# Two fused transformer blocks on one core: layer 0's down product of batches 1 to 3 split into exact fp32r passes, gate weights asked for by ScalarE, next norm moved

## The chip, the cores and the metric

One core of a Trainium2 chip runs the whole program. The metric is the device time of one execution in microseconds (us). Three runs of the kernel before took 1489.95, 1476.10 and 1484.36 us, median 1484.36.

## The reference, cut to what matters

Four batches of 512 tokens with 512 features go through two layers. In each, `x = x + attention(norm(x)) * silu(ffn(norm(x)))`. Layer 0 is what changes:

```python
xn = layernorm(x)
s = softmax_attention(xn) @ Wo                 # 32 query heads, 8 key heads, head size 16
h = silu(xh @ W_gate.T * sg) * (xh @ W_up.T * su)   # xh = Hadamard(xn * SU_ug), 2048 wide
y = Hadamard(h * SU_dp) @ W_down.T * sd        # 2048 -> 512: the "down product"
x = x + s * silu(y)
```

Layer 1 has a gated delta-rule recurrence with six heads of 64 as its attention, and an FFN whose weights are signs. It is not changed. The Hadamard transforms are folded into the weights on the chip, so that the down product of one batch is a 2048 by 512 matrix `wdn` times the hidden `hT` (features by tokens, 16 tiles of 128x512).

## The kernel before

**Units.** Layer 0 is a loop over units u = 0 to 267 (`for u in range(NU + LAG + 1)`, NU = 256, LAG = 11, LATE = 16). A unit takes one step of every stage:

- `maxima(u)` (L461, L462): two score matmuls into the one PSUM buffer "sc", and a DVE reduction of them to row maxima.
- `exps(u - 11)` (L486, L488): two transposed score matmuls into the one PSUM buffer "st", and one ACT exponential of 128x1024.
- work that earlier units postponed with `later(n, f)`, n units on.
- at u % 8 = 3, `values` (L496, L502 to L521): sixteen matmuls of probabilities by values into "y". The row sums go through DRAM (L503, L505), DVE inverts them (L509), they come back spread out (L510, L512), POOL multiplies (L516), and four copies place the result (L521).
- two halves of an FFN unit v = u - 16.
- at set units: query rows (L475, L477), queries (L423, L427, copied by L448), the layer sum of the batch before (`layer_sum`, L534 to L539), its second norm (stats1, `norm1_turn` L568 to L571), and for the next batch `load_x`, norm0 (stats0 L137, root L146 to L154, scale L73, turn L166, copy L167), `keys` (L319, L322, L328) and `values_of` (L341, L346).

**FFN units.** A batch b has 64 of them. In the first 32 (`gate_up`) each unit makes one half of a 128x512 tile of gate or up: eight fp32r matmuls (L363), four 128-row parts of the features by a high and a low half of the weights. ACT takes the tanh of the gate (L370), DVE makes the silu (L371, one unit later), ACT copies the up product into `hT` (L374) and POOL multiplies the two (L375). In the other 32 (`down`) each unit makes two fp32 matmuls (L382) of a 128-token slice of `hT` by `wdn[:, c]`. After sixteen of them ACT takes a tanh (L386) and DVE writes the gate `g0` (L387), tokens by features. FFN units run 16 behind u, so in the loop's own count r = u % 64 the down units stand at r = 48 to 63 and 0 to 15, and the gate units at r = 16 to 47. The text calls them the down stretch and the gate stretch. After u = 255 one half goes to each unit, and what remains of batch 3 (`rest`) is mixed with the first projections of layer 1.

**Weights.** Batch 0 folds the weights as it goes (`fos`) and stores the gate and up weights, split in two, in DRAM (`wS`). For batches 1 to 3 `gate_weights` (L579) loads one 512 KB tile "wc" for each gate unit, three units ahead, through SP's queue; four buffers. `wdn` stays in SBUF and is folded by `fold_down` (L301, L302).

**Order.** From u = 48 `keep_order()` ties every instruction of PE, DVE, ACT and POOL to the one before it on its engine, in the order in which the Python code issues them. SP, which issues nearly all DMAs, is not tied by it; its queue is in order, and an issue waits for its data there.

**PSUM.** "mm" has three buffers, "sc", "st" and "y" one each. `misc()` gives "y" to values, query rows, queries, keys, values_of, the norms' transposes and layer_sum.

Of the kernel before, what the change touches and what calls it, by code (L numbers as in the profile page):

```python
# [10 lines left out]
F32 = mybir.dt.float32  # L11
# [19 lines left out]
EPS = 1e-5  # L31
GUESS = 1597463007.0
# [3 lines left out]
def kernel(ctx: ExitStack, tc: tile.TileContext, i: dict, out: bass.AP):  # L36
# [53 lines left out]

    identf = new(cst, [P, P], F32, "identf")
# [9 lines left out]
    if True:  # L101
# [10 lines left out]
        wdn = new(awp, [P, NI, DM], F32, "wdn")  # L112
# [81 lines left out]
        stage = [new(hp, [P, DM], F32, "hT", bufs=16) for _ in range(NI)]  # L194
# [93 lines left out]
        def mix_down(q):  # L288
# [4 lines left out]
            if q == NI - 1:  # L293
                for o in range(4):
                    nc.sync.dma_start(
                        wdn[:, ts(o, 4), :], wdt[ts(o, DM), :].rearrange("(a p) n -> p a n", p=P)
                    )

        def fold_down(a):
            ph = misc()  # L300
            nc.tensor.matmul(ph, hmat, wdn[:, a, :], start=True, stop=True)  # L301
            nc.vector.scalar_tensor_tensor(wdn[:, a, :], ph, cdn[:, a : a + 1], drow, ALU.mult, ALU.mult)  # L302
# [53 lines left out]
        def gate_up(b, c, m, part):  # L356
# [15 lines left out]
            else:  # L372
                hT = hTs[b, c] = new(hp, [P, SEQ], F32, "hT", bufs=16)
                nc.scalar.copy(hT, pgs[1])  # L374
                nc.gpsimd.tensor_tensor(hT, hT, ths[b, c], ALU.mult)  # L375

        def down(b, t, c):
# [4 lines left out]
            nc.tensor.matmul(ys[t], hTs[b, c][:, ts(t, P)], wdn[:, c, :], start=(c == 0), stop=(c == NI - 1))  # L382
# [5 lines left out]

        def ffn(u, part):
            b, r = u // 64, u % 64  # L390
            if r < 32:
                gate_up(b, r // 2, r % 2, part)
            else:
                down(b, (r - 32) // 8, 2 * (r % 8) + part)
# [135 lines left out]
        def layer_sum(b, t):  # L530
            tok = ds((b * TB + t) * P, P)
            ps = misc()
            for k in range(KC):
                nc.tensor.matmul(ps, oTs[b, k][:, ts(t, P)], wo[:, k, :], start=(k == 0), stop=(k == KC - 1))  # L534
            def place():
                sg = new(zp[0], [P, DM], F32, "sg")
                nc.vector.scalar_tensor_tensor(sg, ps, 0.5, g0s[b][:, t, :], ALU.mult, ALU.mult)
                x1 = x1s[t] = new(zp[0], [P, DM], F32, "x1", bufs=4)
                nc.gpsimd.tensor_tensor(x1, sg, xins[b][:, t, :], ALU.add)  # L539
                nc.sync.dma_start(x1_d[tok, :], x1)  # L540
# [34 lines left out]
        def gate_weights(p):  # L575
            b, r = p // 64, p % 64
            if 0 < b < NB and r < 32:
                w = wcs[b, r // 2, r % 2] = new(zp[0], [P, 2, KC, P], F32R, "wc", bufs=4)
# [1004 lines left out]
```

## Time and profile before

| | |
|---|---|
| runs | 1489.95, 1476.10, 1484.36 us; median 1484.36 |
| profiled execution | 1483.26 us, of which the span on the core is 1481.5 |
| mean granted TensorE clock | 0.990 |
| PE busy | 1413.0 us (95%) |
| DVE, ACT, POOL busy | 1039.4, 691.0, 313.9 us |
| batch 1: gate stretch, down stretch | 265.91 to 361.96, 361.96 to 441.96 us |
| batch 2 | 441.96 to 534.32, 534.32 to 615.78 us |
| batch 3 | 615.78 to 706.14; layer 1's first matmul at 778.02 us |
| DMA | 199.10 MB, mean 134 GB/s |

How lines of the profile are read. A group has the line, the engine, the operation, output<-inputs by the program's names, shapes and a count; then the busy time and the mean ns of one; then the idle time of the engine just before them and what ended it. A timeline line has the start, the length, the engine, the line and the count of instructions drawn together, and in brackets the idle time before it with what ended it. PE is TensorE's matmuls, PEld its weight loads; SPq is SP's sequencer, which issues DMAs. "DMA share" is the mean busy share of the core's 16 DMA engines.

### The profile page before, as it was taken

To read this page: it belongs to the slowest core of one execution; us is meant where nothing else is said; L and a number is where in the kernel's file an instruction comes from. 1 tells how busy PE (TensorE), PEld (TensorE's weight loads), DVE (VectorE), ACT (ScalarE), POOL (GpSimd) and SP (SyncE) were. 2 spreads that over 40 slices of the span, in tenths; PEclk is the share of its full clock that TensorE was granted. 3 is DMA by queue.
4 is the path that set the end of the run, shared out by engine and by line. 5 is a ranking of instruction groups with operands and counts; after the bars stand their busy time and mean duration, and the time that the engine had idled before them with its cause. 6 is when DMAs were issued, how large, how long until landed. Compare 5 with 4: busy or idle time off the path is not lost.

```text
span 1481.5 us, 22721 instructions
## 1 busy us (share of the span) xinstructions
PE 1413.0 (95%) x8144; PEld 856.0 (58%) x8144; DVE 1039.4 (70%) x1926; ACT 691.0 (47%) x1027; POOL 313.9 (21%) x304
## 2 busy tenths in 40 slices
PE   7989999989999999999999799999999999999898
PEld 3555533555335643466334566777568766776675
DVE  7999755767557755676517769677965799477646
ACT  4654454556445664566443424423442345323433
POOL 1122200323004210133111220054112531152001
PEclk9999999999999999999999999999999999999989
DMA  8865220465006730266024443434462354425532
GB/s 304 329 224 191 101 73 23 160 228 193 25 23 210 236 132 25 74 226 212 20 61 124 149 114 100 131 77 149 126 177 83 97 155 134 128 72 153 157 82 96
DMA packets 201792, 199.10 MB, mean 134 GB/s; under 512 B 65520, under 2 KB 153040, under 8 KB 200784
## 3 DMA queue, kind: packets, MB, share of 16 engines
q1 hardware_dynamic: 198624, 196.29, 42.0%
q10 hardware_dynamic: 3056, 1.37, 0.4%
q8 instruction: 64, 1.05, 0.3%
q14 instruction: 48, 0.39, 0.1%
HBM read 146.80 MB, written 46.19 MB: 130 GB/s over the span
## 4 chain that ended last, share of the span: by engine, by line
PE 64%; DVE 22%; DMA 5%; issue 4%; ACT 3%; SPq 1%; POOL 1%; POOLq 0%; ACTq 0%; DVEq 0%
PE mm L382 15%; PE mm L363 12%; PE ph L1066 5%; PE sc L461 4%; PE y L1097 4%; DVE yc L844 2%; DVE UT L1200 2%; PE pu L885 2%; DVE sx L1196 2%; DVE nmx L462 2%; PE pu L836 1%; PE pu L1157 1%; PE pu L1333 1%; PE pu L1306 1%; PE pu L1394 1%
## 5 line engine op out<-in xcount | busy, mean ns | idle before, releaser
L462 DVE TENSOR_REDUCE nmx<-sc 128x2 f32<-128x1024 f32 x256 | 312.7, 1222 | 194.4 <-PE st L486 192.4
L488 ACT ACTIVATE pe<-st 128x1024 f16<-128x1024 f32 x256 | 262.3, 1024 | 158.9 <-PE st L486 157.9
L382 PE MATMUL mm<-wdn,hT 128*128 128x512 f32 x512 | 253.5, 618 | 0.0
L363 PE MATMUL mm<-xr,wc 128*128 128x512 f32 x768 | 205.6, 410 | 7.5 <-DMA wc<-wS 7.2
L363 PEld LDWEIGHTS mm<-xr,wc 128*128 128x128 f32 x768 | 138.5, 190 | 57.8 <-issue 27.4
L375 POOL TENSOR_TENSOR hT<-hT,th 128x512 f32<-128x512 f32 x64 | 84.9, 1326 | 291.2 <-ACT hT L374 285.2
L382 PEld LDWEIGHTS mm<-wdn,hT 128*128 128x128 f32 x512 | 87.0, 189 | 93.4 <-issue 93.1
L836 PE MATMUL pu<-xn1T,wp 128*128 128x512 f32 x288 | 131.2, 599 | 0.0
L1066 PE MATMUL ph<-xsh,sg 128*128 128x512 f32 x256 | 113.7, 444 | 6.0 <-ACT sg L1051 5.7
L516 POOL TENSOR_TENSOR oT<-os,sm 128x512 f16<-128x512 f32 x32 | 41.3, 1292 | 313.8 <-DMA sm<-rec_d 222.9
L1051 ACT ACTIVATE sg<-sw 128x512 fp32r<-128x512 f32 x128 | 79.5, 625 | 56.3 <-PE y L1097 29.0
L1066 PE MATMUL ph<-xsl,sg 128*128 128x512 f32 x256 | 104.9, 410 | 0.7 <-DVE xsl L1026 0.7
L461 PE MATMUL sc<-kT,qT 32*128 32x512 f16 x512 | 99.6, 385 | 5.9 <-DVE nmx L462 5.6
L486 PE MATMUL st<-qm,kT 32*128 32x512 f16 x512 | 100.3, 386 | 0.2 <-ACT pe L488 0.2
L461 PEld LDWEIGHTS <-qT 32*128 32x128 f16 x512 | 25.4, 91 | 120.7 <-issue 115.1
L1071 ACT ACTIVATE hT<-ph,upsc 128x512 f32<-128x512 f32 x64 | 43.8, 684 | 94.2 <-PE ph L1066 94.0
L836 PEld LDWEIGHTS pu<-xn1T,wp 128*128 128x128 f32 x288 | 54.0, 192 | 56.3 <-issue 54.7
L1097 PE MATMUL y<-sg,hsh 128*128 128x512 f32 x256 | 83.3, 434 | 0.6 <-ACT sg L1051 0.6
L1144 POOL TENSOR_TENSOR gm<-g,le 128x384 fp32r<-128x384 f32 x64 | 56.8, 905 | 87.1 <-PE pu L1145 54.7
L363 PE MATMUL mm<-xr,fo 128*128 128x512 f32 x256 | 73.8, 421 | 1.1 <-DVE fo L277 1.1
L1097 PE MATMUL y<-sg,hsl 128*128 128x512 f32 x256 | 73.5, 400 | 0.0
L370 ACT ACTIVATE th<-mm,hwg 128x512 f32<-128x512 f32 x64 | 44.0, 688 | 63.1 <-PE mm L363 63.1
(311 smaller groups left out, 2355.6 us busy)
## 6 DMA issues: line engine op xcount, KB each, us to landing
wc<-wS SPq DMA_DIRECT2D x96, 512.0 KB
wS<-fo SPq DMA_DIRECT2D x16, 1024.0 KB
sw<-in_upT SPq DMA_DIRECT2D x64, 256.0 KB
sw<-in_downT SPq DMA_DIRECT2D x64, 256.0 KB
sm<-rec_d SPq DMA_DIRECT2D x128, 64.0 KB
raw<-in_w_gateT SPq DMA_DIRECT2D x8, 512.0 KB
hT<-in_w_downT SPq DMA_DIRECT2D x16, 256.0 KB
raw<-in_w_upT SPq DMA_DIRECT2D x8, 512.0 KB
```

Of the source, the lines that this page charges most:

```text
L363: nc.tensor.matmul(pgs[m], wcs[b, c, m][:, h, k, :], xrs[b][:, k, :], start=(k + h == 0), stop=(k == KC - 1 and h == 1))
L375: nc.gpsimd.tensor_tensor(hT, hT, ths[b, c], ALU.mult)
L382: nc.tensor.matmul(ys[t], hTs[b, c][:, ts(t, P)], wdn[:, c, :], start=(c == 0), stop=(c == NI - 1))
L461: nc.tensor.matmul(sc[:, j, :], qTs[n][rows, ts(t, P)], kTs[b, g // 4][rows, :], start=True, stop=True)
L462: nc.vector.tensor_reduce(nmxs[n][:, t, 2 * pr : 2 * pr + 2], sc, AX.X, ALU.max, negate=True)
L486: nc.tensor.matmul(st[:, j, :], kTs[b, g // 4][rows, ts(k, P)], qms[n][rows, :], start=True, stop=True)
L488: nc.scalar.activation(pes[u], st, AF.Exp)
L836: nc.tensor.matmul(pp, wps[b, n][:, k, 0:P], xn1Ts[b][:, k, :], start=(k == 0), stop=(k == KC - 1))
L1051: tc.keep_in_program_order(nc.scalar.activation(sgs[b, c, m], raws[b, c, m], AF.Sign))
L1066: ins = nc.tensor.matmul(ph, sgs[b, c, 0][:, ts(k, P)], xss[b][n][:, k, :], start=(k + n == 0), stop=(k == KC - 1 and n == 1))
L1097: ins = nc.tensor.matmul(yss[b][t], hss[b, c][n][:, ts(t, P)], sgs[b, c, 1], start=(c + n == 0), stop=(c == NI - 1 and n == 1))
L1144: nc.gpsimd.tensor_tensor(gm, bc_in(s["g2"][:, t, u, x], P), bc_mid(le, 3), ALU.mult)
```

## The change

It touches layer 0 only.

1. *Down product of batches 1 to 3.* Each 128x128 by 128x512 product in fp32 becomes three passes in fp32r: two in "A" (Wh by Hh, and Wl by Hl, where Wh and Wl are the high and low parts of the weights, Hh that of `hT`, and Hl its low part times 4096), one in "B" (Wl - Wh/4096 by Hh - Hl). A times 1 + 1/4096, plus B, is the whole product. The result has features by tokens. The weights come from two new DRAM arrays, `wA` and `wB`, in 24 tiles of 512 KB a batch, through the "wc" buffers. `down_product` asks for the tile it begins and for the next two, on ACT's queue; the first request of a batch stands directly ahead of its first product. The order of the 192 passes is a fixed list `products`: A for o = 0 and 1; A for o = 2 and 3 together, with B for o = 0 six steps behind (the "joint part"); then the rest of B. While A of o = 3 goes on, DVE subtracts low from high in each of the sixteen `hT` pairs.
2. *Split of `hT`* in the gate stretches of batches 1 to 3. ACT copies the up product, scaled, into "cut"; POOL multiplies (one unit later); DVE masks off low bits in `truncate` (two later); ACT writes the high part and POOL the low part (three later). "hT" gets 32 buffers, and `wdn` becomes sixteen of them.
3. *Batch 0's down stretch* stays in fp32 and makes the parts of the weights: `down_parts`, sixteen times.
4. *layer_sum* of batches 1 to 3 is transposed as well, and the new `token_sum` turns its result with four fp32 transposes and adds x on DVE (POOL for batch 0).
5. *Moved steps.* norm0 of the next batch from r = 36 to 52 to r = 48 to 59, its four stats in two units; `keys` from r = 49 to 60; `values_of` from r = 52, 53, 57, 60 to r = 1, 2, 5, 6 of its own batch; `load_x` from r = 26 to 32; queries seven units ahead instead of ten, their copies four instead of eight; second norm of the batch before by three to six units.
6. *Gate weights* are asked for by ACT instead of SP, with five buffers instead of four.

The diff, cut:

```diff
@@ -88 +89 @@
 
     wdt = new(dram, [FF, DM], F32, "wdt")
 
+    wA = new(dram, [KC, NI // 4, P, 4, 2, P], F32, "wA")
+    wB = new(dram, [KC, NI // 8, P, 8, P], F32, "wB")
+
@@ -191 +194 @@
-        stage = [new(hp, [P, DM], F32, "hT", bufs=16) for _ in range(NI)]
+        stage = [new(hp, [P, DM], F32, "hT", bufs=2 * NI) for _ in range(NI)]
+        wdn = [new(hp, [P, DM], F32, "hT", bufs=2 * NI) for _ in range(NI)]
@@ -291 +295 @@
             if q == NI - 1:
-                for o in range(4):
-                    nc.sync.dma_start(
-                        wdn[:, ts(o, 4), :], wdt[ts(o, DM), :].rearrange("(a p) n -> p a n", p=P)
-                    )
+                for a in range(NI):
+                    nc.sync.dma_start(wdn[a], wdt[ts(a, P), :])
 
         def fold_down(a):
             ph = misc()
-            nc.tensor.matmul(ph, hmat, wdn[:, a, :], start=True, stop=True)
-            nc.vector.scalar_tensor_tensor(wdn[:, a, :], ph, cdn[:, a : a + 1], drow, ALU.mult, ALU.mult)
+            nc.tensor.matmul(ph, hmat, wdn[a], start=True, stop=True)
+            nc.vector.scalar_tensor_tensor(wdn[a], ph, cdn[:, a : a + 1], drow, ALU.mult, ALU.mult)
+
+        def down_parts(a):
+            cut = new(zp[0], [P, DM], I32, "xn1")
+            nc.vector.tensor_scalar(cut, wdn[a].bitcast(I32), -4096, None, ALU.bitwise_and)
+            cut = cut.bitcast(F32).rearrange("p (o n) -> p o n", o=KC)
+            hl = new(zp[0], [P, KC, 2, P], F32R, "wc", bufs=5)
+            low = new(zp[0], [P, KC, P], F32R, "xo")
+
+            def halves_of():
+                nc.scalar.copy(hl[:, :, 0, :], cut)
+                nc.gpsimd.tensor_tensor(
+                    hl[:, :, 1, :], wdn[a].rearrange("p (o n) -> p o n", o=KC), cut, ALU.subtract
+                )
+
+            def difference():
+                nc.vector.scalar_tensor_tensor(low, cut, -CUT, hl[:, :, 1, :], ALU.mult, ALU.add)
+                nc.sync.dma_start(
+                    wA[:, a // 4, :, a % 4].rearrange("o p f n -> p o (f n)"),
+                    hl.bitcast(F32).rearrange("p o f n -> p o (f n)"),
+                )
+                nc.sync.dma_start(wB[:, a // 8, :, a % 8].rearrange("o p n -> p o n"), low.bitcast(F32))
+
+            later(1, halves_of)
+            later(3, difference)
 
@@ -369 +395 @@
                 pg = pgs[0]
                 nc.scalar.activation(th, pg, AF.Tanh, scale=hwg[:, c : c + 1])
                 later(1, lambda: nc.vector.scalar_tensor_tensor(th, th, 1.0, pg, ALU.add, ALU.mult))
-            else:
-                hT = hTs[b, c] = new(hp, [P, SEQ], F32, "hT", bufs=16)
+            elif b == 0:
+                hT = hTs[b, c] = new(hp, [P, SEQ], F32, "hT", bufs=2 * NI)
                 nc.scalar.copy(hT, pgs[1])
                 nc.gpsimd.tensor_tensor(hT, hT, ths[b, c], ALU.mult)
+            else:
+                cut, t = new(hp, [P, SEQ], F32, "cut"), ths[b, c]
+                nc.scalar.activation(cut, pgs[1], AF.Copy, scale=1.0 / CUT)
+
+                def truncate():
+                    nc.vector.tensor_scalar(cut.bitcast(I32), t.bitcast(I32), -4096, None, ALU.bitwise_and)
+
+                def halves_of():
+                    hi, lo = hTs[b, c] = [new(hp, [P, SEQ], F32R, "hT", bufs=2 * NI) for _ in range(2)]
+                    nc.scalar.activation(hi, cut, AF.Copy, scale=CUT)
+                    nc.gpsimd.tensor_tensor(lo, t, cut, ALU.subtract)
+
+                later(1, lambda: nc.gpsimd.tensor_tensor(t, cut, t, ALU.mult))
+                later(2, truncate)
+                later(3, halves_of)
 
         def down(b, t, c):
...
-            nc.tensor.matmul(ys[t], hTs[b, c][:, ts(t, P)], wdn[:, c, :], start=(c == 0), stop=(c == NI - 1))
+            nc.tensor.matmul(ys[t], hTs[b, c][:, ts(t, P)], wdn[c], start=(c == 0), stop=(c == NI - 1))
...
+        dws = {}
+
+        def down_weights(b, n):
+            if n < 16:
+                w = new(zp[0], [P, 4, 2, P], F32R, "wc", bufs=5)
+                nc.scalar.dma_start(w.bitcast(F32), wA[n // 4, n % 4])
+            else:
+                w = new(zp[0], [P, 8, P], F32R, "wc", bufs=5)
+                nc.scalar.dma_start(w.bitcast(F32), wB[(n - 16) // 2, n % 2])
+            dws[b, n] = w
+
+        def tile_of(kind, o, c, f):
+            return 4 * o + c // 4 if kind == "A" else 16 + 2 * o + c // 8
+
+        AHEAD = 6
+        products = [("A", o, c, f) for o in range(KC - 2) for c in range(NI) for f in range(2)]
+        for c in range(NI + AHEAD):
+            if c < NI:
+                products += [("A", o, c, f) for o in range(KC - 2, KC) for f in range(2)]
+            if c >= AHEAD:
+                products.append(("B", 0, c - AHEAD, 0))
+        products += [("B", o, c, 0) for o in range(1, KC) for c in range(NI)]
+        uses = list(dict.fromkeys(tile_of(*x) for x in products))
+
+        def request(b, at):
+            for n in uses[at : at + 3]:
+                if (b, n) not in dws:
+                    down_weights(b, n)
+
+        begun = set()
+
+        def down_product(b, i):
+            kind, o, c, f = products[i]
+            n = tile_of(kind, o, c, f)
+            if (b, n) not in begun:
+                begun.add((b, n))
+                request(b, uses.index(n))
+            if i == 0:
+                g0s[b] = new(zp[0], [P, KC, SEQ], F32, "g0", bufs=1)
+            if c + f == 0:
+                ys[kind, o] = new(bmm, [P, SEQ], F32, "mm")
+            g, y = g0s[b][:, o, :], ys[kind, o]
+            if kind == "A":
+                nc.tensor.matmul(y, dws[b, n][:, c % 4, f, :], hTs[b, c][f],
+                                 start=(c + f == 0), stop=(c == NI - 1 and f == 1))
+                if f == 1 and c == NI - 1:
+                    nc.scalar.activation(g, y, AF.Copy, scale=1.0 + CUT)
+                if f == 1 and o == KC - 1:
+                    hi, lo = hTs[b, c]
+                    later(1, lambda: nc.vector.tensor_tensor(hi, hi, lo, ALU.subtract))
+                return
+            nc.tensor.matmul(y, dws[b, n][:, c % 8, :], hTs[b, c][0], start=(c == 0), stop=(c == NI - 1))
+            if c == NI - 1:
+                th = new(hp, [P, SEQ], F32, "th")
+
+                def add():
+                    nc.vector.tensor_tensor(g, y, g, ALU.add)
+                    nc.scalar.activation(th, g, AF.Tanh, scale=0.5)
+
+                later(1, add)
+                later(2, lambda: nc.vector.scalar_tensor_tensor(g, th, 1.0, g, ALU.add, ALU.mult))
+
         def ffn(u, part):
             b, r = u // 64, u % 64
             if r < 32:
                 gate_up(b, r // 2, r % 2, part)
+            elif b == 0:
+                down(b, (r - 32) // 8, 2 * (r % 8) + part)
             else:
-                down(b, (r - 32) // 8, 2 * (r % 8) + part)
+                if r == 32 and part == 0:
+                    request(b, 0)
+                for n in range(3):
+                    down_product(b, 3 * (2 * (r - 32) + part) + n)
 
         def misc(dtype=F32):
 
@@ -528 +636 @@
         def layer_sum(b, t):
-            tok = ds((b * TB + t) * P, P)
             ps = misc()
             for k in range(KC):
-                nc.tensor.matmul(ps, oTs[b, k][:, ts(t, P)], wo[:, k, :], start=(k == 0), stop=(k == KC - 1))
+                if b == 0:
+                    nc.tensor.matmul(ps, oTs[b, k][:, ts(t, P)], wo[:, k, :], start=(k == 0), stop=(k == KC - 1))
+                else:
+                    nc.tensor.matmul(ps, wo[:, k, ts(t, P)], oTs[b, k], start=(k == 0), stop=(k == KC - 1))
+            g = g0s[b][:, t, :]
+            later(1, lambda: nc.vector.scalar_tensor_tensor(g, ps, 0.5, g, ALU.mult, ALU.mult), True)
+
+        def token_sum(b, t):
+            x1 = x1s[t] = new(zp[0], [P, DM], F32, "x1", bufs=4)
+            x1_out = x1_d[ds((b * TB + t) * P, P), :]
+            if b == 0:
+                nc.gpsimd.tensor_tensor(x1, g0s[b][:, t, :], xins[b][:, t, :], ALU.add)
+                nc.sync.dma_start(x1_out, x1)
+                return
+            ps = misc()
+            for k in range(KC):
+                nc.tensor.transpose(ps[:, ts(k, P)], g0s[b][:, k, ts(t, P)], identf)
+
             def place():
-                sg = new(zp[0], [P, DM], F32, "sg")
-                nc.vector.scalar_tensor_tensor(sg, ps, 0.5, g0s[b][:, t, :], ALU.mult, ALU.mult)
-                x1 = x1s[t] = new(zp[0], [P, DM], F32, "x1", bufs=4)
-                nc.gpsimd.tensor_tensor(x1, sg, xins[b][:, t, :], ALU.add)
-                nc.sync.dma_start(x1_d[tok, :], x1)
+                nc.vector.tensor_tensor(x1, ps, xins[b][:, t, :], ALU.add)
+                nc.sync.dma_start(x1_out, x1)
 
             later(1, place, True)
 
@@ -575 +696 @@
         def gate_weights(p):
             b, r = p // 64, p % 64
             if 0 < b < NB and r < 32:
-                w = wcs[b, r // 2, r % 2] = new(zp[0], [P, 2, KC, P], F32R, "wc", bufs=4)
-                nc.sync.dma_start(w.bitcast(F32), wS[r // 2, r % 2])
+                w = wcs[b, r // 2, r % 2] = new(zp[0], [P, 2, KC, P], F32R, "wc", bufs=5)
+                nc.scalar.dma_start(w.bitcast(F32), wS[r // 2, r % 2])
 
...
             if u % 8 == 0 and 0 < u <= NU:
                 query_rows(u // 8 - 1)
-            if u % 32 in (22, 23) and u + 10 < NU:
-                queries((u + 10) // 64, (u + 10) % 64 // 32, u % 32 - 22)
-            if u % 8 == 0 and u + 8 < NU:
+            ahead = 7 if u >= FIRST else 10
+            if u % 32 - 32 + ahead in (0, 1) and u + ahead < NU:
+                queries((u + ahead) // 64, (u + ahead) % 64 // 32, u % 32 - 32 + ahead)
+            if u % 8 == (4 if u >= FIRST else 0) and u + 8 - u % 8 < NU:
                 set_queries(u // 8 + 1)
             if 16 <= v < 16 + NI:
                 fold_down(v - 16)
+            if 32 <= v < 64 and v % 2 == 0:
+                down_parts((v - 32) // 2)
             if 0 < b < NB and r in (18, 19, 20, 21):
                 layer_sum(b - 1, r - 18)
             if 0 < b < NB:
-                if 21 <= r < 25:
-                    stats1(b - 1, r - 21)
-                if 25 <= r < 28:
-                    root_of((b - 1, 1), zp[0], mvs[b - 1], r - 25)
-                if 28 <= r < 32:
-                    norm1_turn(b - 1, r - 28)
-                if 27 <= r < 31:
-                    norm1_scale(b - 1, r - 27)
+                if r in (22, 23, 27, 28):
+                    token_sum(b - 1, (22, 23, 27, 28).index(r))
+                if r in (24, 25, 29, 30):
+                    stats1(b - 1, (24, 25, 29, 30).index(r))
+                if 30 <= r < 33:
+                    root_of((b - 1, 1), zp[0], mvs[b - 1], r - 30)
+                if r in (34, 35, 36, 37):
+                    norm1_turn(b - 1, (34, 35, 36, 37).index(r))
+                if 33 <= r < 37:
+                    norm1_scale(b - 1, r - 33)
+                if r in (1, 2, 5, 6):
+                    values_of(b, ((1, 2, 5, 6).index(r),))
             if b + 1 < NB:
-                if r == 26:
+                if r == 32:
                     load_x(b + 1)
-                if 36 <= r < 40:
-                    stats0(b + 1, r - 36)
-                if 40 <= r < 43:
-                    root_of(b + 1, b0, lnp[b + 1], r - 40)
-                if 44 <= r < 48:
-                    norm0_turn(b + 1, r - 44)
-                if 43 <= r < 47:
-                    norm0_scale(b + 1, r - 43)
-                if r in (48, 49, 50, 52):
-                    norm0_copy(b + 1, (48, 49, 50, 52).index(r))
-                if r == 49:
+                if r in (48, 49):
+                    for t in range(2 * r - 96, 2 * r - 94):
+                        stats0(b + 1, t)
+                if r == 50:
+                    root_of(b + 1, b0, lnp[b + 1], 0)
+                if r == 51:
+                    root_of(b + 1, b0, lnp[b + 1], 1)
+                    root_of(b + 1, b0, lnp[b + 1], 2)
+                if 52 <= r < 56:
+                    norm0_turn(b + 1, r - 52)
+                if 51 <= r < 55:
+                    norm0_scale(b + 1, r - 51)
+                if 56 <= r < 60:
+                    norm0_copy(b + 1, r - 56)
+                if r == 60:
                     keys(b + 1)
-                if r in (52, 53, 57, 60):
-                    values_of(b + 1, ((52, 53, 57, 60).index(r),))
```

More of the change, by code (lines that the diff above doesn't have):

```diff
@@ L31 @@
 EPS = 1e-5
+CUT = 2.0**-12
 GUESS = 1597463007.0
@@ L110 @@
         a0 = top.enter_context(tc.tile_pool(name="a0", bufs=1, side="right"))
-        wdn = new(awp, [P, NI, DM], F32, "wdn")
         su_ug = new(awp, [P, KC], F32, "su_ug")
@@ L692 @@
         rest.append((free,))
-        rest += [(layer_sum, NB - 1, t) for t in range(TB)]
+        rest += [(f, NB - 1, t) for f in (layer_sum, token_sum) for t in range(TB)]
         rest += [(stats1, NB - 1, t) for t in range(TB)]
```

## The prediction

> **What bounds the kernel now.** I read the page first (shares of the span, then the costliest groups), then the stretches of one batch, then the timeline of one step in each, then the waits and the chain that ended last. The page:
>
> ```profile
> PE 1413.0 (95%) x8144; PEld 856.0 (58%) x8144; DVE 1039.4 (70%) x1926; ACT 691.0 (47%) x1027; POOL 313.9 (21%) x304
> ...
> L382 PE MATMUL mm<-wdn,hT 128*128 128x512 f32 x512 | 253.5, 618 | 0.0
> L363 PE MATMUL mm<-xr,wc 128*128 128x512 f32 x768 | 205.6, 410 | 7.5 <-DMA wc<-wS 7.2
> ```
>
> PE is busy 95% of 1481.5 us, and the down products (L382, fp32, two records to a product) are its largest group. The stretches of batch 1 (us, then busy time of PE, PEld, DVE, ACT, POOL, then granted clock, DMA share, GB/s), with one of batch 0 ahead:
>
> ```profile
> 111.00:148.00 37.00, 35.08 (x168) 22.14 (x167) 36.91 (x57) 17.91 (x25) 8.05 (x6) 1.00 0.54 191
> ...
> 333.00:370.00 37.00, 37.00 (x204) 21.94 (x200) 28.20 (x50) 24.44 (x34) 11.19 (x9) 0.97 0.56 193
> ...
> 407.00:444.00 37.00, 37.00 (x163) 13.78 (x162) 22.01 (x26) 18.32 (x20) 2.53 (x2) 1.00 0.09 23
> ```
>
> Gate stretches move 193 GB/s, down stretches 23. From batch 1 on PE is full and DVE and ACT have room; batch 0's gate stretch is DVE's (36.91 of 37). One plain down unit:
>
> ```profile
> 399.22 0.39 PE L461 MATMUL sc<-kT,qT 32*128 32x512 f16 x2
> ...
> 399.55 1.98 PE L382 MATMUL mm<-wdn,hT 128*128 128x512 f32 x4
> ...
> 401.46 0.39 PE L461 MATMUL sc<-kT,qT 32*128 32x512 f16 x2
> ```
>
> A unit takes 401.46 − 399.22 = 2.24: scores and exps 0.32, two products 1.92. A plain gate unit takes 2.37, of which eight fp32r passes are 2.05. What PE waits for in a gate stretch, and what SP was doing:
>
> ```profile
> 328.90 3.75 PE L363 MATMUL mm<-xr,wc 128*128 128x512 f32 x8 [3.54 <-DMA wc<-wS]
> ...
> 333.13 2.99 PE L363 MATMUL mm<-xr,wc 128*128 128x512 f32 x8
> ```
>
> ```profile
> 495.38 2.47 SPq L521 DMA_DIRECT2D oTc<-oT  x4
> ...
> 497.90 2.48 SPq L448 DMA_DIRECT2D qT<-qd  x4
> ...
> 500.49 1.00 SPq L579 DMA_DIRECT2D wc<-wS  x2
> ...
> 503.95 1.39 PE L363 MATMUL mm<-xr,wc 128*128 128x512 f32 x5 [2.56 <-DMA wc<-wS]
> ```
>
> SP's queue stood five us in two groups of small copies; only then was the tile asked for, and it needed 3.33 us (the chain's figure there; 3.33 to 3.43 at four such places). After the 3.54 wait the same eight passes take 3.75, then 2.99, against 2.12: the granted clock is 0.5 from 328.20 for 6.83 us. After the 2.56 wait it stays full.
>
> **The change part by part.** The sum starts from the profiled run, 1483.26 (span 1481.5 and 1.8 around it), 1.1 below the median 1484.36.
>
> *Passes.* Per unit two fp32 products (1.91) become six fp32r passes. L363's eight take 2.04, so six take 1.53: −0.38 a unit, 96 units: **−36.5**.
>
> *Gate tiles asked for by ACT, five buffers.* The three large waits go (7.2), with what the half clock cost: 7.62 + 3.47 for two units that should take 4.74, less the 3.54 counted, 2.8. **−10.0**; 0 if ACT asks as late as SP. The Trainium skill ("DMA: Bandwidth & Descriptors", "Issuing engines are not separate DMA queues") speaks against it: all issuers share the same 16 engines, so another issuer saves only issue time. By that alone this term is 0 and the sum ten higher; the rows above put the delay ahead of the issue, in SP's queue, so I keep the row.
>
> *Next norm and values_of moved.* In batch 0 stats (four of 0.67 + 0.18 = 3.4), thirteen roots (2.4) and 0.7 of scale leave the full DVE: −6.5. Their four turns on PE (0.24 each) now stand where PE is full, +1.0: **−5.5** (+1.0 to −5.5). DVE has 15 of 37 us free in the down stretch that they enter, four stats in two units (1.7 each): hidden there. For batches 2 and 3 the turns only change from one full stretch to another: 0. values_of now stands at r 1, 2, 5, 6 beside values at u%8 = 3, and both use the single bank "y". The nearest row is a 1.28 wait of PE for DVE's vp in batch 2: 3 × 1.28 = **+3.8** (0 to 6.9, three of 2.3). The other moves keep their work and change units: load_x, six units later in SP's queue, is still 16 units (36 us) ahead of the first stats; the query copies (four L448 issues a set) come four units before their set instead of eight, some 9 us for 2.5 of issue and a landing like the tiles' 3.4; SP has lost 96 issues of 0.3 ahead of them. keys, eleven units later, leaves its kT copies four units before the first scores, so a copy behind L521's or L448's 2.5 could cost 0 to 1 a batch; taken as 0, by that 9 us.
>
> *Splitting hT.* Per two gate units ACT has two exps (2.05), tanh 0.69 and the cut 0.59 as before, and a new hi copy 0.59: 3.9 of 4.74. DVE gains a 0.42 truncate on 28.2 of 37; POOL goes from 1.3 to 2.6 of 4.74. Covered by PE: 0; without that cover see the last rival. The Trainium skill ("SBUF — State Buffer", the shared port pair) says DVE and GpSimd lock each other out for whole instructions. Some rows look so (L375 median 1291, longest 1852), and 48 such delays of 0.56 would be 27; the sum takes none of it, since POOL's slack is larger than that.
>
> *Batch 0's down_parts.* Sixteen times a mask and a scalar_tensor_tensor on DVE (0.4 to 0.7 and 0.69), a copy on ACT (0.59), a subtract on POOL (1.29) and two stores: every second unit (4.48) of a stretch where DVE is busy 20 of 37. 0.
>
> *First weight tiles.* For each of batches 1 to 3 ACT asks for the first down tile in the unit that multiplies with it. The nearest rows are the tile loads: 3.4 from issue to PE, some 0.3 more for ACT to reach it: 3.7, between 3.4 and 6.6, since three tiles go out together and 512 KB at 330 GB/s (228 at a share of 0.69, the stretch from 296 to 333) is 1.6 each. The 3.7 is as long as the wait that halved the clock, which then costs 1.7 (3.41 us at half, as after a 3.06 wait at 812.76) to 2.8: (3.7 + 1.7) × 3 = **+16.2** (10 to 28).
>
> Later tiles are asked for two ahead, at eight passes (2 us) each and 3.4 to land. Twenty-four of them in some 65 us are 193 GB/s, what a gate stretch carries now: no further wait is taken, and one a batch (1.1 to 2.6, as on wc without a drop of the clock) would be 3 to 8.
>
> *Joint part.* In some eleven units sixteen hi−lo subtracts (0.69, L1026's median for such a tile) join DVE: its work there is 27.9, PE's 23.4. +4.3 to 5 in batches 1 and 2, less if a wait of PE elsewhere lets DVE catch up: **+8.6** (0 to 10). In batch 3 it lies in the tail.
>
> *token_sum.* Four sets of four fp32 transposes per batch, 0.44 a set (a unit with L568's is that much longer): 12 × 0.44 = **+5.3**. The final add goes from POOL to DVE, 0.69, hidden.
>
> *Tail.* In the last eleven units, without maxima, the one "st" bank gives a cycle of 1.5 (exp begins 0.53 after its scores and lasts 1.02); before, 2.24 of PE covered it. Now PE has some 12.2 in 16.5: +4.3, and +2 for the added chain (add, tanh, multiply, transposes) where layer 1 begins: **+6.3** (2 to 8).
>
> Sum: −36.5 − 10.0 − 5.5 + 3.8 + 16.2 + 8.6 + 5.3 + 6.3 = −11.8: **1471**.
>
> **The rivals.**
> - *Covers hold* (chance 0.20). The clock stays full after the first-tile waits (3 × 3.4 = 10.2, so −6), DVE's excess is half made up (−4.3), "y" never blocks (−3.8) and the tail costs 2 (−4.3): −18.4, 1453. For it: 2.56 did not halve the clock, and 1.28 is the only such wait. Against it: 3.4 lies near 3.54.
> - *The gain is eaten* (0.13). The down stretch does not reach 1.86 a unit, because exps and reduces, each with one bank, and DVE pace it: at 2.05 half of the passes' gain goes (+18), 1489. For it: exp ends 1.55 after the unit's start, 0.31 before the next. Against it: a reduce of 1.22 leaves DVE a third of the unit.
> - *ACT's queue is the bound* (0.25, the other side). In it stand now 96 gate and 72 down requests, and an exp behind a request waits with it. If the 0.35 of an issue does not run beside ACT's own work, two gate units need 3.9 + 0.7 and 0.44 for the copies of os, queries and xo (twelve of 0.59 on sixteen pairs): 5.05 against 4.74, +0.31 × 16 × 3 = +15. And SP's gate requests waited for PE 21.4 (20 times) and 15.4 (22 times), 36.8; half of it on ACT, five buffers against four, is +18: 1504. It decides from 0.17 a request (1499.2 − 1471.5 over 168). Against it: ACT's own DMA issues in layer 1 start 0.05 after the instruction ahead of them (835.18, 835.23).
> - *No gain in fp32r at all* is excluded by L363's passes on tiles of the same shape.
>
> **How the numbers follow.** The remaining 0.42 is my sum, itself 1457 to 1485 (first tiles 10 to 28, joint 0 to 10). One per cent, about what a measurement of this kernel can tell from no change, is 1469.5 and 1499.2. The sum stands close above the lower bound, which cuts it in about half: 0.22 faster, 0.20 same. With covers holding: faster 0.42. Same: 0.20 and the eaten gain 0.13: 0.33. ACT's queue: slower 0.25. The range runs from 1449, the first rival with the rest of the joint part made up too (−4.3), to 1504, the third.
>
> **What would show it.** The plain down unit of batches 1 to 3 at 1.86; no gate wait over a us on wc; at the start of each down stretch a PE wait of 3.4 to 6.6 on a weight tile and then a lower clock; in the joint part PE waiting on DVE's hT; at u%8 = 3 early in a batch PE waiting on vp; batch 0's gate stretch some six us shorter; exps closer together than PE's work in the tail. It is wrong if ACT's queue shows waits ahead of exps, if down units stay at 2.05 or more, or if first tiles land at once.

## The result and the profile after

The changed kernel takes 1600.39 us (median of four runs, 1594.75 to 1603.64) against 1485.34 before (four runs): ratio 1.0786, 95% interval 1.0735 to 1.0836. It is slower by some 115 us, where 1471 was forecast. The profiled execution has a span of 1600.3 us, and the mean granted clock is 0.958 instead of 0.990. The page of the changed kernel:

```profile
PE 1432.8 (90%) x8384; PEld 917.2 (57%) x8384; DVE 1111.4 (69%) x2078; ACT 732.0 (46%) x1103; POOL 380.4 (24%) x356
...
PEclk9999998989999989999999999999999999999989
...
L389 PE MATMUL mm<-xr,wc 128*128 128x512 f32 x768 | 217.1, 428 | 0.0
L473 PE MATMUL mm<-hT,wc 128*128 128x512 f32 x384 | 119.1, 436 | 14.0 <-DMA wc<-wA 14.0
```

The 7.2 us of waits on gate tiles (wS) are gone, and 14.0 on the new weight tiles (wA) have come. PE's busy time has not fallen: the down passes are shorter, but matmuls on PE ran at a lower clock for part of the time. Per pass, L389 takes 428 ns where the same work took 410.

Where the time went is seen from the start of each unit's score matmul, by stretches of units (us, worked out from both timelines; the last column runs from u = 255 to the end of the span):

| | u 0-47 | batch 0 down, 48-79 | gate 1 | down 1 | gate 2 | down 2 | gate 3 | u 240-254 | rest |
|---|---|---|---|---|---|---|---|---|---|
| before | 166.9 | 80.0 | 96.0 | 80.0 | 92.4 | 81.5 | 90.4 | 36.0 | 739.3 |
| after | 163.2 | 98.4 | 121.5 | 93.0 | 112.2 | 94.1 | 110.2 | 36.5 | 752.9 |

The three gate stretches lose 65, the down stretches of batches 1 and 2, where the passes were to gain, lose 26, batch 0's down stretch 18, and the rest 14. The last fifteen down units, which the passes alone should shorten, did not gain either: the first tile's wait (3.53 there) stands in them.

The gate stretches of batches 2 and 3 lose most at two places, r = 34 and 42. Batch 1 loses at the same two, and still more at r = 18 and 25 (units of 9.99 and 11.22 against 3.25 and 2.37). The timeline of the changed kernel at u = 98, which is r = 34 of batch 1 (start, length, engine, line; idle before in brackets):

```profile
350.53 1.26 POOL L624 TENSOR_TENSOR oT<-os,sm 128x512 f16<-128x512 f32 x1 [8.66 <-DMA sm<-rec_d]
351.75 1.26 POOL L412 TENSOR_TENSOR hT<-th,cut 128x512 fp32r<-128x512 f32 x1
...
352.97 1.26 POOL L414 TENSOR_TENSOR th<-cut,th 128x512 f32<-128x512 f32 x1
353.05 0.69 ACT L396 ACTIVATE th<-mm,hwg 128x512 f32<-128x512 f32 x1 [6.20 <-POOL hT L412]
...
353.63 1.02 ACT L596 ACTIVATE pe<-st 128x1024 f16<-128x1024 f32 x1
...
354.70 0.61 PE L594 MATMUL st<-qm,kT 32*128 32x512 f16 x2 [4.24 <-ACT pe L596]
...
355.24 3.78 PE L389 MATMUL mm<-xr,wc 128*128 128x512 f32 x8
```

It is read from the top. POOL stands 8.66 us before oT, until sm has come back from DRAM. The low half (L412) is queued behind it, and it reads th; so ACT's next tanh, which writes th's buffer, stands 6.20; the exp behind the tanh on ACT is late; and PE, whose next transposed scores need the one bank that exp reads, stands 4.24. Then the clock drops: eight passes take 3.78 instead of 2.12. The unit takes 9.74 instead of 2.37.

The lists of waits say the same for the whole program (who waited for whom: us in total, times, longest). The kernel before, then the changed one:

```profile
POOL oT L516 <- DMA sm<-rec_d: 222.9, 23, 20.0
```

```profile
POOL oT L624 <- DMA sm<-rec_d: 319.3, 28, 25.2
...
ACT th L396 <- POOL hT L412: 47.5, 9, 7.2
...
PE st L594 <- ACT pe L596: 26.6, 14, 4.5
```

Before, ACT's list has no wait for POOL, and PE's waits on ACT's exp of layer 0 come to 0.2. The buffers say why the low half is so close to ACT. "th" and "cut" have two buffers each. Before, POOL read th in the unit of its up product, three units ahead of the tanh that takes the buffer again. Now its last reader, the low half, stands three units later, in the unit of that tanh itself, with no unit to spare.

The same queue stops PE in batch 0's down stretch, at r = 2:

```profile
236.08 1.26 POOL L624 TENSOR_TENSOR oT<-os,sm 128x512 f16<-128x512 f32 x1 [9.64 <-DMA sm<-rec_d]
237.29 1.26 POOL L315 TENSOR_TENSOR wc<-hT,xn 128x512 fp32r<-128x512 f32 x1
...
238.49 0.95 POOL L362 MEMSET vp<- 128x1024 f16 x1
239.48 0.29 DVE L372 CAST vp<-y 128x128 f16<-128x128 f32 x1 [5.04 <-POOL vp L362]
...
239.83 0.60 PE L367 MATMUL y<-wv,xnT 128*128 128x128 f16 x4 [4.73 <-DVE vp L372]
```

values_of begins with a memset of vp on POOL. Moved to r = 1, it stands behind oT and down_parts' subtract; DVE's copy waits for it, the bank "y" for the copy, and PE for the bank.

### The profile page after: what moved, and what is told of

The parts are those of the page before. It is cut to its first block, busy times and chain, and to the rows that moved or that the text cites. A ratio compares the mean times of both kernels' runs of the same rounds, so it can differ in the third digit from the quotient of the medians.

```text
span 1600.3 us, 23680 instructions
## 1 busy us (share of the span) xinstructions
PE 1432.8 (90%) x8384; PEld 917.2 (57%) x8384; DVE 1111.4 (69%) x2078; ACT 732.0 (46%) x1103; POOL 380.4 (24%) x356
## 5 line engine op out<-in xcount | busy, mean ns | idle before, releaser
L389 PE MATMUL mm<-xr,wc 128*128 128x512 f32 x768 | 217.1, 428 | 0.0
L389 PEld LDWEIGHTS mm<-xr,wc 128*128 128x128 f32 x768 | 145.7, 200 | 54.2 <-issue 25.2
L473 PE MATMUL mm<-hT,wc 128*128 128x512 f32 x384 | 119.1, 436 | 14.0 <-DMA wc<-wA 14.0
L594 PE MATMUL st<-qm,kT 32*128 32x512 f16 x512 | 103.0, 397 | 26.8 <-ACT pe L596 26.6
L624 POOL TENSOR_TENSOR oT<-os,sm 128x512 f16<-128x512 f32 x32 | 41.8, 1306 | 351.7 <-DMA sm<-rec_d 319.3
L473 PEld LDWEIGHTS mm<-hT,wc 128*128 128x128 f32 x384 | 71.6, 200 | 46.1 <-issue 17.7
L412 POOL TENSOR_TENSOR hT<-th,cut 128x512 fp32r<-128x512 f32 x48 | 61.4, 1279 | 118.6 <-DVE cut L407 118.6
L569 PEld LDWEIGHTS <-qT 32*128 32x128 f16 x512 | 26.6, 91 | 108.7 <-issue 99.4
L396 ACT ACTIVATE th<-mm,hwg 128x512 f32<-128x512 f32 x64 | 44.0, 688 | 87.8 <-POOL hT L412 47.5
L389 PE MATMUL mm<-xr,fo 128*128 128x512 f32 x256 | 73.5, 424 | 3.3 <-DVE fo L281 3.3
```

The lines of the kernel that those rows point to most:

```text
L389: nc.tensor.matmul(pgs[m], wcs[b, c, m][:, h, k, :], xrs[b][:, k, :], start=(k + h == 0), stop=(k == KC - 1 and h == 1))
L412: nc.gpsimd.tensor_tensor(lo, t, cut, ALU.subtract)
L473: nc.tensor.matmul(y, dws[b, n][:, c % 4, f, :], hTs[b, c][f], start=(c + f == 0), stop=(c == NI - 1 and f == 1))
L569: nc.tensor.matmul(sc[:, j, :], qTs[n][rows, ts(t, P)], kTs[b, g // 4][rows, :], start=True, stop=True)
L594: nc.tensor.matmul(st[:, j, :], kTs[b, g // 4][rows, ts(k, P)], qms[n][rows, :], start=True, stop=True)
```

## The experiments

Theory A: POOL's in-order queue. It waits for sm as it did before, but now it holds steps that ACT, DVE and PE need at once. Theory B: ACT's queue, which holds the weight requests. Theory C: the 50 MB more of DMA traffic. Medians are set against the 1600.39 of the changed kernel; ratios are to the kernel before, from the same chip.

**1. oT without the sums.**

```diff
-nc.gpsimd.tensor_tensor(oT, os_, sm, ALU.mult)
+nc.gpsimd.tensor_tensor(oT, os_, os_, ALU.mult)
```

> Leaves out the division by the row sums: POOL multiplies os by itself in the step oT (L624), so that it no longer waits there for sm's way through DRAM; the copies of sums and inverses still run. Theory A (POOL's in-order queue is the new bound: oT waits there for sm, and the new POOL steps behind it, hT low half, th times cut, the vp memset and down_parts' subtract, are waited for by ACT, DVE and PE): the six waits of PE on ACT's pe at r = 34 and 42 (3.5 to 4.5 us, units of 7.7 to 9.8 instead of some 2.6, so 33 together), the wait of 7 at u = 89, the wait of 6 at u = 82 and some 5 to 8 before vp go: 1540 to 1555 against 1600. Theory B (ACT's queue, which now holds the weight requests, is the bound): within 10 of 1600. Theory C (the added 50 MB of DMA traffic slow every copy, and the clock with it): within 15 of 1600.

1533.25 (ratio 1.0335, 1.0281 to 1.039): 67 less, with one operand of one POOL step changed. Gate stretches 97.6, 97.2 and 99.7, the clock 0.975. PE's waits on ACT's exp fall from 26.6 to 2.9, and the six units at r = 34 and 42 of the three batches alone give back 38 of the 67. The run also lets SP copy oT, and layer_sum read it, sooner (9.99 to 5.76 at u = 82), so the 67 are what the wait for sm costs by all its ways. The weight traffic is the same, so C is not the main cause. The down stretches of batches 1 and 2 stay at 93.1 and 92.0.

**2. values_of earlier.**

```diff
-if r in (1, 2, 5, 6): values_of(b, ((1, 2, 5, 6).index(r),))
+if r == 1: values_of(b, (3,))
+if 61 <= r < 64: values_of(b + 1, (r - 61,))
```

> values_of of the next batch goes back into the batch before: tiles 0 to 2 at r = 61, 62, 63, tile 3 at r = 1, so the vp memset stands on POOL ten units earlier, away from values at r = 3. Theory A: the stall at r = 2 and 3 (units of 7.58 and 8.23, 3.64 and 6.44, 4.40 and 7.18 us in the three batches, against some 2.2 and 3.1) shrinks to at most 2 us a batch: 1580 (1573 to 1590). Theory B: no change, 1595 to 1605. Theory C: no change.

1593.04 (1.0738, 1.0673 to 1.0804): a third of what was expected, and its interval overlaps that of the changed kernel (1.0735 to 1.0836). The stretches say more: batch 0's down stretch gave 7.1; in batches 1 and 2 other waits took the place (figures of batch 1: DVE's kd 0.93, vp 1.26, 0.55 and 0.55 on the same bank at r = 61 to 64, then 1.05 on exp and 0.70 and 1.23 on a subtracted hT at r = 6 and 7).

**3. First tile early.**

```diff
 if r < 32:
+    if b > 0 and part == 0 and r >= 29: ahead_request(b, r - 29)
```

> The first three weight tiles of each down stretch are asked for in the last three gate units (r = 45, 46, 47 of the loop), one each, instead of directly ahead of the first product. All theories: PE's wait of 3.45 to 3.66 at r = 48 goes, and the half clock after it: 12 us less (8 to 16), 1588. If theory B holds strongly, the requests only move the wait and less than 5 is gained.

1594.24 (1.0747, 1.0682 to 1.0811): half of it, again with an overlapping interval. The wait on the tile is gone (its unit takes 2.15 instead of 7.35), and three units later PE waits 3.86 for DVE's nmx, because DVE waits for POOL: what the tile's wait had covered. The timeline of this run:

```profile
402.91 1.29 POOL L630 TENSOR_TENSOR oT<-os,sm 128x512 f16<-128x512 f32 x1 [5.40 <-DMA sm<-rec_d]
...
406.72 0.43 DVE L407 TENSOR_SCALAR cut<-th 128x512 int32<-128x512 int32 x1 [2.37 <-POOL th L414]
...
410.25 0.39 PE L575 MATMUL sc<-kT,qT 32*128 32x512 f16 x2 [3.86 <-DVE nmx L576]
```

**4. Requests on SP.** The three weight loads with `nc.sync.dma_start` instead of `nc.scalar.dma_start`.

> All weight requests of gate and down stretches go back from ACT's queue to SP's. Theory B: ACT is freed, 1570 or less. Theory A: ACT's queue was not the cause; SP's queue takes 168 more issues and the sums' way gets longer, so POOL's waits grow: 1600 to 1640. Theory C: within 15 of 1600.

1567.31 (1.0565): 33 less, as B said and A did not. But the run does not set B apart from A: POOL's waits for sm became shorter too (319.3 to 260.5), where A expected them to grow, and ACT's waits for the low half with them (47.5 to 36.4). The first down units fall from 7.35, 7.16 and 7.00 to 2.2, since SP is not tied to PE's order and asks early, yet the down stretches as a whole gain 0.7 each: other waits take the place. The gain stands in the gate stretches (22) and behind u = 255 (7).

**5. oT two units later.** `later(5, place)` becomes `later(7, place)`; layer_sum, token_sum and the second norm follow.

> The whole computation. POOL's step oT stands seven units after values instead of five in every queue; layer_sum starts at r = 20 instead of 18, token_sum at 27, the second norm one unit later. Theory A (POOL waits in its queue for sm, PE's work behind it): sm lands 13 to 22 us after os, five gate units are 12 to 15 us and seven 17 to 20, so most of POOL's wait goes and with it four fifths of the 67 us that the first experiment gave: 1545 to 1560. Theory B (ACT's queue): 1595 to 1605.

1557.83 (1.0488): 42.6 less, with the whole computation. Gate stretches 100.0, 102.0, 100.8.

**6. No subtraction.** The `later(1, ...)` with DVE's hi minus lo is left out.

> Leaves out DVE's sixteen subtractions of low from high a batch (B is then multiplied by the high part alone), nothing else. The prediction put the DVE excess of the joint part at 4.3 to 5 a batch for two batches: 1590 (1585 to 1593). Rival: the loss at r = 63 to 3 comes from the one bank y, held until vp is copied, and the subtractions cost nothing: 1597 to 1603.

1619.8 (1.0906): no gain at all; the down stretches stay (92.5 and 94.9). That the run is 19 slower, mostly in gate stretches, is not explained. In the changed kernel PE waits for a subtracted hT only twice, 1.2 in all, so the forecast price of the joint part was not there to be had.

**7. Before, gate requests by ACT.** `bufs=5` and `nc.scalar.dma_start` in gate_weights, nothing else.

> The kernel before with one part of the change alone: gate tiles asked for by ACT, five buffers instead of four. The prediction's term: the waits of PE on wc (7.2) and the half clock after them (2.8) go, 1474 against 1484, ratio 0.993. Theory A: POOL is not in PE's way in this kernel, so the slightly later sums cost nothing: the same 1474. Theory B (requests on ACT hold the exps back): 1490 or more, since moving them to SP took 33 off the changed kernel.

1501.48, ratio 1.0106 (1.0072 to 1.014): 15 slower where 10 faster was forecast. The six runs lie between 1490.01 and 1507.59, and the profiled one is the fastest, so its rows explain at most some 7 of the 15. In it no wait on wS is left, as forecast. In its place stands one that the kernel before does not have:

```profile
PE y L534 <- DMA oTc<-oT: 9.0, 6, 3.1
```

It is layer_sum, which reads the sums' result; its first units (u = 82, 146 and 210) take 6.13, 6.90 and 6.69 instead of 3.25. The sums come later. The timeline of this run ahead of u = 146:

```profile
437.10 0.33 ACTq L579 DMA_DIRECT2D wc<-wS  x1
...
440.62 0.34 SPq L510 DMA_DIRECT2D rec_d<-rc  x1
...
444.31 1.72 SPq L512 DMA_DIRECT2D sm<-rec_d  x4
...
449.79 1.28 POOL L516 TENSOR_TENSOR oT<-os,sm 128x512 f16<-128x512 f32 x1 [22.16 <-DMA sm<-rec_d]
...
454.23 0.38 PE L534 MATMUL y<-wo,oTc 128*128 128x512 f16 x1 [3.09 <-DMA oTc<-oT]
```

And the same set in the kernel before:

```profile
439.32 0.34 SPq L510 DMA_DIRECT2D rec_d<-rc  x1
...
440.75 1.93 SPq L512 DMA_DIRECT2D sm<-rec_d  x4
...
444.45 0.34 SPq L579 DMA_DIRECT2D wc<-wS  x1
...
444.66 1.29 POOL L516 TENSOR_TENSOR oT<-os,sm 128x512 f16<-128x512 f32 x1 [18.22 <-DMA sm<-rec_d]
```

From the store of the inverses to oT it is 5.34 before and 9.17 here. Before, the first tile of the stretch is asked for behind the sums' copies, in the same queue; here ACT has asked for four tiles between 437.10 and 443.82, ahead of them. That these loads slow the copies is argued from the order of the rows; no run held it alone. ACT waits in this run as well, in rows that the kernel before does not have ("ACT th L370 <- DMA oTc<-oT: 13.1, 6, 2.7", though ACT's tanh needs nothing of oTc), but PE waited only 2.2 for ACT's exp and 1.7 for one of its copies. What ties ACT to those landings, the trace does not show.

**8. Three moves** (5, 2 and 3 together).

> The whole computation: oT seven units after values, values_of at r = 61, 62, 63 and 1, first weight tiles asked for three units early, together. Theory A: with POOL's wait gone the other two stalls are no longer covered by it and count in full: 45 to 55 from oT, 10 to 15 from values_of, 10 to 15 from the first tiles: 1515 to 1535. If the stalls only take each other's place, 1545 or more.

1543.28 (1.0391): 57 less, between the two forecasts, near the second: stalls partly took each other's place.

**9. Moves alone.** The kernel before, with norm0, keys, values_of, load_x and queries at their new places.

> The kernel before with the moves alone: norm0, keys, values_of, load_x and the queries at the places of the changed kernel; down products in fp32, requests on SP, second norm unmoved. The prediction's terms: norm0 out of batch 0's gate stretch -5.5, y and vp +3.8: 1482, ratio 0.999. Theory A: the vp memset stands behind oT on POOL at r = 1 to 3, and PE waits on y for vp; the changed kernel lost some 10 us in each of the three places: 1495 to 1512.

1490.17, ratio 1.0034 (1.002 to 1.0048): 5 slower, between the sum's 1482 and theory A's 1495. Up to u = 47 it gains 7.4 and in batch 1's gate stretch 5.1, and its down stretches lose 8.9, 7.2 and 4.7; in batch 1's PE waits 1.96 and 1.51 on vp.

**10. Passes without moves.**

> The changed kernel with norm0, keys, values_of and load_x back at their places of before; passes, split, token_sum and requests on ACT stay. Theory A: the stalls at r = 0 to 6 go (8 to 10 a batch), batch 0's gate stretch gets its 5 back, the gate stretches get norm0's DVE work on top of the split's: 1570 to 1590. Rival (the moves are needed, since DVE is full in the gate stretch with the split): 1600 or more.

1603.33 (1.0797): nothing, in the rival's range. Batch 0's down stretch falls to 87.8, but the gate stretches stay at 120.9, 118.3 and 111.6. The moves are not the main cause, and undoing them does not help while oT stands on POOL.

**11 and 12. All repairs** (8 with 4), **and without the moved norm0, keys, values_of.**

> The whole computation: oT seven units after values, values_of at r = 61 to 63 and 1, first tiles early, and all weight requests back on SP. Theories A and B add up if both hold: 1543 of the three moves less 15 to 33: 1510 to 1528. If SP's requests only shortened the wait of oT for sm, which is gone by then: 1538 to 1548.

> As the run with all repairs, but norm0, keys, values_of and load_x at their places of before. What is left of the change is then the passes, the split, token_sum and the weight parts: 1495 to 1515, if the stalls in the down stretch come from the moved steps; as the run with all repairs or above, if they come from the passes themselves.

1529.08 (1.0297) and 1529.9 (1.0303). SP's requests give 14 on top of the three moves, so they are not only a shorter wait of oT: PE's waits on ACT's exp fall from 11.9 in run 8 to 2.4. This is what theory B is worth with most of POOL's part out of the way. Run 12 is no faster than run 11; by its forecast the stalls that are left come from the passes, not from the moved steps. The down stretches still do not gain (86.1 and 88.6; 82.8 and 81.8), and this is their new wait, from run 12:

```profile
395.98 0.25 DVE L623 RECIPROCAL rc<-rc 128x16 f32<-128x16 f32 x1 [3.74 <-DMA rc<-sum_d]
...
397.56 0.39 PE L575 MATMUL sc<-kT,qT 32*128 32x512 f16 x2 [3.08 <-DVE nmx L576]
```

DVE's reciprocal is postponed by three units. Three units of 1.91 instead of 2.24 are a microsecond less, and the copies it waits for stand in SP's queue with the weight tiles; so DVE stops, and PE's scores behind it (theory D).

**13 and 14. Reciprocal five units and oT nine units after values**, two buffers for os; with the moves and without.

> The whole computation, all repairs, and in addition: DVE's reciprocal of the row sums stands five units after values instead of three, oT nine units after (seven for a batch's last set), os has two buffers. Theory D (work postponed by a count of units comes too early now that a unit is shorter and the copies slower: DVE stands on rc, and PE's scores behind it): the waits of PE on DVE's nmx in the down stretches (1.8, 2.5, 2.2 us and more a batch, 7 to 10 together) go: 1529 less 20 to 30, so 1499 to 1509. Rival (DVE is simply too full): 1522 to 1532.

> The same with norm0, keys, values_of and load_x at their places of before. Theory D: 1498 to 1510; as the one before within 8, since the moves alone cost 5 in the kernel before. What is then still above before is token_sum, the tail and DVE's work in the gate stretch (norm0 on top of the split), so gate stretches should stay at 100 or more and down stretches fall to 74 to 78 from 80.

1520.74 (1.0255, 1.0232 to 1.0279) and 1512.53 (1.0209, 1.0193 to 1.0224). That is 8 and 17 less than runs 11 and 12, or 6 and 14 by the ratios, less than expected; run 13 lies nearer to the rival's range than to D's. The wait that D names is gone (DVE on rc: 21.3 to 1.7, and 26.8 to none), but these runs move oT and double os as well, so the gain is not the reciprocal's alone. Run 14 is the best with the passes: down stretches 78.6 and 78.0, gate stretches 110.3, 104.3 and 100.5. Nothing beat the kernel before.

## Why the prediction was wrong

**The step that failed** is "Splitting hT": "Covered by PE: 0". It added up POOL's busy time (2.6 of 4.74 us a pair of units) and took the rest for slack. But POOL runs its steps in the order of the code, and the list of waits before already held the row of 222.9 us on sm. That wait cost nothing while what stood behind it was wanted late. The change put behind it two steps that share th and cut, two buffers each, with ACT and DVE, the vp memset and down_parts' subtract, and it moved th's last reader into the unit in which ACT wants the buffer. Taking the wait away from oT gave 67 of the 115. More buffers for th and cut, the other way to loosen the tie, were not tried. The Trainium skill's rule on the shared port ("SBUF — State Buffer", "SBUF: two separate sides") was weighed at this step; it is not where the 67 came from, since run 1 left every step of POOL and DVE in place.

**Passes, −36.5.** Right in kind, a little too large: a plain unit takes some 1.91, in the changed kernel's timeline from one score matmul to the next:

```profile
488.31 0.39 PE L569 MATMUL sc<-kT,qT 32*128 32x512 f16 x2
488.32 0.39 PE L594 MATMUL st<-qm,kT 32*128 32x512 f16 x2
488.64 1.66 PE L481 MATMUL mm<-hT,wc 128*128 128x512 f32 x6
490.23 0.39 PE L569 MATMUL sc<-kT,qT 32*128 32x512 f16 x2
```

490.23 − 488.31 = 1.92, so six passes take 1.59, not 1.53, and a unit saves 0.33 of 2.24: 0.33 × 96 = 32. Most of it was lost again in waits: best down stretch 78.

**Gate tiles by ACT, −10.** Wrong in sign: alone it costs 15 (run 7), and with the down tiles too 33 can be had by going back (run 4). The waits on wS went, as the rows promised; what the reading left out, as far as run 7's rows show, is that SP's late request had let the sums' copies go first. The third rival had the right side, at 0.25, but it stood as an alternative to the sum's terms, not as an addition to another stall, and it put the price on issue time and on waits for PE. That its 33 is also what run 4 gave is luck. The Trainium skill's rule ("DMA: Bandwidth & Descriptors", "Issuing engines are not separate DMA queues") promised nothing but issue time from this part and was nearer than the reading of the rows, though it does not mention the wait.

**Norm and values_of, −5.5 and +3.8.** Batch 0's part was right (−7.4 in run 9, −3.8 here). The other side was too small: alone the moves cost 5 in all, and in the changed kernel r = 2 and 3 together became 5 to 10 longer in each of three batches (7.58 and 8.23 us in batch 0's stretch against 2.24 and 3.22). Two things are in it. At r = 2 it is the memset, which the diff does not touch, but moves: what a moved step issues has to be counted on POOL too, and was not. Without oT's wait (run 1) the unit falls to 2.47, 2.84 and 2.86. At r = 3 it is the bank "y" that the prediction named: values waits 2.1 for DVE's copy of vp in each batch, in run 1 as well, and the unit stays at 5.89 to 7.05 there. With values_of moved away (run 2) it is 3.16 to 3.22. The kind was right and the size, 1.28 a batch, was not.

**First tiles, +16.2.** Measured as forecast, waits of 3.66, 3.45 and 3.53 and units of 7.35, 7.16 and 7.00 against 2.1 to 2.2; but not additive: removing them gave 6 (run 3). Where no further wait was taken, two came, 1.90 and 1.41 on a later tile of wA in batches 1 and 2.

**Joint part, +8.6.** Not there in the changed kernel (run 6), whose other stalls let DVE catch up; PE's waits for a subtracted hT grow from 1.2 to 4.5 in run 2 and 6.4 in run 8, when some of these stalls are gone.

**token_sum and tail, +5.3 and +6.3.** token_sum was not tried alone. The rest from u = 255 is 13.6 longer, 7 to 9 in the repaired runs (11 to 13), 3.3 in run 14; what in it costs that is open.

**What stays open.** Run 14 is 30 above before. Its gate stretches are 10 to 14 longer, much of it at r = 24, 25, 32, 33, 40 and 42, where PE waits on DVE (21.6 on nmx in all), and in batch 1 after a wait of 3.36 on a gate tile at r = 16. Part may be DVE's added work, part the rows below. How much each is was not separated. Nor was the added traffic (theory C) tried alone, as a cause of the sums' later return.

## What to carry to other kernels

An in-order engine's idle time is not slack for new work: look at what it waits for (here 222.9 us on a DMA round trip) and ask who will wait for each instruction put behind that wait, and with how many buffers. Stalls on one loop cover each other, so prices measured one at a time do not add up, and a first repair may show only a fraction. A request that stands late in a queue may be letting something more urgent go first: see what stands ahead of it before it is moved. Delays counted in loop steps shrink in time when the steps get faster; the transfers they cover do not.

## What the runs showed of the hardware

Two small DVE steps took five times their usual time while POOL worked. The timeline of run 11 (the medians of these lines are 0.20 and 0.23):

```profile
510.03 1.29 POOL L412 TENSOR_TENSOR hT<-th,cut 128x512 fp32r<-128x512 f32 x1 [3.88 <-DVE cut L407]
...
510.40 0.98 DVE L581 CAST nm<-nmx 128x16 f16<-128x16 f32 x1
...
511.28 1.28 POOL L414 TENSOR_TENSOR th<-cut,th 128x512 f32<-128x512 f32 x1
511.41 1.23 DVE L582 TENSOR_TENSOR nm<-nmx,nm 128x16 f16<-128x16 f32 x1
```

Each ends about when the POOL instruction beside it ends (510.03 + 1.29 and 511.28 + 1.28). This agrees with the Trainium skill ("SBUF — State Buffer", "SBUF: two separate sides"), by which, for some kinds of DVE operation, one of the two engines blocks for the other's whole instruction. At 515.60 PE waited 2.50 on DVE's nmx, with these two and a chain of small norm steps queued ahead of it. Run 14 has the pair as well (0.96 and 1.26, beside POOL's 1.28 and 1.31).

A wait of PE can cost twice. At the 4.24 wait of 354.70 the granted clock went to 0.5 for 6.83 us, and eight passes took 3.78 against 2.12. Over the whole program the mean granted clock fell from 0.990 to 0.958; without POOL's wait it was 0.975, in run 14 0.986. The length of the wait alone does not tell: at the 2.50 wait in run 11, with one of 0.56 ahead of it, the clock went to 0.5 for 3.41 us, and at the 2.56 wait in the kernel before it stayed full.
